# A four-layer adaptive transformer stack in fp32: layers 0 and 1 by halves of the tokens, layer 1's low-rank maps multiplied ahead, and attention's first steps placed among them

## The chip, the core and the metric

The kernel runs on one core of one Trainium2 chip. A core has a matrix engine (TensorE, "PE" in the profile, with its weight loads as "PEld"), three elementwise engines (VectorE "DVE", ScalarE "ACT", GpSimd "POOL") and DMA queues. Each engine works through its own list of instructions in order; semaphores tie them together. Matrix products land in PSUM, eight banks of 128 partitions x 512 fp32 numbers; everything else lies in SBUF. The metric is device time in microseconds of one execution.

## What is computed

There are 8 sequences of 128 tokens with 512 features, so 1024 tokens. Four layers each add to x:

```python
x = x + L0_ffn(L0_cond(x, itok_B_2_6))     # gated MLP with low-rank terms, then routed experts
x = x + L1_ffn(L1_cond(x, itok_B_3_7))     # low-rank map per sequence, then soft-routed experts
x = x + L2_ffn(L2_cond(x, table, lens))    # attention over a paged cache, then a dense layer
x = x + L3_ffn(L3_cond(x, itok_B_0_7))     # routed experts, then 64 small experts

def L0_cond(x): # F = 1376, rank 16, per-sequence A, B
    gate = x @ Wg.T + 0.5 * (x @ Ag.T) @ Bg.T
    up   = x @ Wu.T + 0.5 * (x @ Au.T) @ Bu.T
    h = silu(gate) * up
    return h @ Wd.T + 0.5 * (h @ Ad.T) @ Bd.T

def L0_ffn(x):  # 8 experts of rank 16, the best 2 of them
    w = top2_normalised(softmax(x @ router.T))
    mid = einsum('bsd,edr->bser', x, A) * w[..., None]
    return x @ base.T + 2 * einsum('bser,erd->bsd', mid, B)

def L1_cond(x, ids): return (x @ B[ids].T) @ A[ids].T            # rank 16
def L1_ffn(x):  # 8 experts of rank 16, all of them
    scores = 8 * softmax(x @ Wr.T + br)
    return 2 * einsum('bshr,hor,bsh->bso', einsum('bsd,hrd->bshr', x, A), B, scores)

def L2_cond(x): # 32 query heads, 8 key heads of 128, 512 cached keys + 128 new ones
    q, k = rope(rmsnorm(x @ Wq.T)), rope(rmsnorm(x @ Wk.T)); v = x @ Wv.T
    p = softmax(mask(q @ concat(k_cache[table], k).T / sqrt(128)))
    return (p @ concat(v_cache[table], v)) @ Wo.T
```

L3_cond has the form of L0_ffn with a bias on the logits.

## The kernel before

x is kept transposed, 128 partitions x 4 chunks x 1024 tokens. `TG` = 2 halves of 512 tokens, `NB` = 8 blocks of 128, `DC` = 4 chunks of features, `NF` = 11 chunks of the hidden size. `mm` is one matmul; all matmuls in the profile show the line of such a helper. Tiles come from pools; a pool with `bufs=1` has one buffer for a tag, so the next tile of this tag has to wait until the last one is read. Instructions of an engine can be moved against each other by the scheduler, within their dependencies.

The down projection runs over all tokens for two output chunks at a time, with its low-rank term after the first pair:

```python
for o in range(0, DC, 2):
    wd = st.tile([P, NF, 2 * P], F32, tag="wd", name=f"wd_{o}")      # and its load
    banks = [bank(f"dn_{o}_{j}") for j in range(4)]                   # four quarters of the tokens
    for k in range(2):
        for j in range(4):
            for f in range(NF):
                mmq(banks[j][:, k, :], wd[:fw, f, k * P : (k + 1) * P], h[:fw, f, quarter(j)], ...)
    if o == 0:
        lora_down()                                                   # td, tdm
    ... mmq(banks[j][:, k, :], Bd[...], tdm[slot(j), :], False, True)
    for j in range(4):
        act.copy(y0[:, o : o + 2, quarter(j)], banks[j])
```

The experts of layers 0, 1 and 3 are one function over all 1024 tokens (shortened):

```python
def experts(sm, ps_pool, yT, wmr, tag, topk, mult, bias, wB, base, evac):
    for j in range(NB // 2):
        ps = ps_pool.tile([P, 2, 136], F32, tag="mm", name=f"mid_{tag}_{j}")
        for i in range(2):
            for c in range(DC):
                mm(ps[:, i, :], yT[:, c, t0 : t0 + P], wmr[:, c, :], c == 0, c == DC - 1)
        dve.tensor_copy(lg[:, 2 * j : 2 * j + 2, :], ps[:, :, 128:136])   # or + bias
        mids.append(ps)
    dve.tensor_reduce(mx, lg, AX.X, ALU.max)
    dve.tensor_tensor(e, lg, mx..., ALU.subtract)
    act.activation(e, e, AF.Exp)
    if topk:                          # rank of each of the 8 against the other 8: r1, r2, rank
        ...
    ...                               # s: sum, scale, reciprocal; e * s
    for g in range(TG):
        pt = ps_pool.tile([P, 512], F32, tag="mm", name=f"midTp_{tag}_{g}")
        for j in (2 * g, 2 * g + 1):
            dve.tensor_tensor(mw, mids[j][:, :, 0:128], e..., ALU.mult)
            for i in range(2):
                pe.transpose(pt[:, o : o + P], mw[:, i, :], ident)
        act.copy(midT[:, g * 512 : (g + 1) * 512], pt)
    for o in range(DC):
        for g in range(TG):
            ps = ps_pool.tile([P, 512], F32, tag="mm", name=f"eo_{tag}_{o}_{g}")
            if base is not None:
                for c in range(DC):
                    mm(ps, base[:, c, o * P : (o + 1) * P], yT[:, c, tok], c == 0, False)
            mm(ps, wB[:, o * P : (o + 1) * P], midT[:, tok], base is None, True)
            evac(o, tok, ps)          # add_to_x on VectorE, or a copy
```

Layer 1 follows layer 0, and attention follows layer 1:

```python
experts(sm, psp, y0, wmr0, "l0", "probs", 2.0, None, wB0, base0, add_to_x)
for g in range(TG):
    for c in range(DC):
        mm(ps, wa1[:, c, :], x[:, c, tok], c == 0, c == DC - 1)           # t
    block_masked(t1[:, tok], ps, mask1, g)
    for o in range(DC):
        mm(ps, wb1[:, o * P : (o + 1) * P], t1[:, tok], True, True)       # y
        act.copy(y1[:, o, tok], ps)
experts(sm, psp, y1, wmr1, "l1", None, 16.0, br..., wB1, None, add_to_x)
sp.dma_start(kept, x)
y2 = attention(tc, a, x, ident, lens, kvrow, part, ww, ypool, sums, rows, chunks, mm)
```

Attention has 32 steps (4 groups of heads x 8 sequences) with two key heads each, behind a set-up of sines and cosines (`rotary`). In a step:

```python
def gather(n):      # POOL: 4 + 4 indirect DMAs
    kn = kvp.tile([P, 4, nk], F32, tag="kn", name=f"kn_{n}")              # bufs=2
    ...             # cached keys into kn, cached values into vals[n % 2]
def rope(src, n, nh, tabs, tag):
    t = wk.tile(..., tag="ra" + n); u = wk.tile(..., tag="rb" + n)        # bufs=2
    dve.tensor_tensor(t, src, ws..., ALU.mult)
    for lo, hi in ((0, 64), (64, 0)):
        pool.tensor_tensor(u[:, :, lo : lo + 64], src[:, :, hi : hi + 64], wx..., ALU.mult)
    dve.tensor_tensor(t, t, u, ALU.add)
    return t
def project(n):
    ...             # POOL: four table products ts, tx of sine and cosine with the norm weights
    ...             # kv and two q products, copies, squares (sq), sums of squares (ssq)
    act.activation(rs, ssq, AF.Sqrt, bias=eps, scale=1.0 / HD); dve.reciprocal(rs, rs)
    ...             # k and q times rs
    S[n]["k"] = rope(k1, "k", ...); S[n]["q"] = [rope(t, "q", ...) for t in qs]
def turn(n):
    ...             # kTc: cached keys transposed, copied to kT by DVE; kTn: the new keys
    ...             # qTp: queries transposed, copied to qT by ACT          (bufs=4)
def weigh(n, g):    # st: kT x qT, exp on ACT into pT
def mix(n, g, pT):  # av: pT x vals; sums: reciprocal of the row sum; o, on DVE
def leave(n, g, o): # oTp: o transposed, oT on ACT, wo product, added to y2 on DVE

weights(0); gather(0); project(0); turn(0)
last = None
for n, (qd, b) in enumerate(steps):
    for g in range(GK):
        pT = weigh(n, g)
        o = mix(*last) if last else None
        if more and g == 0:
            gather(n + 1); project(n + 1)
        if more and g == 1:
            turn(n + 1)
        if last:
            leave(*last[:2], o)
        last = (n, g, pT)
```

In PSUM, attention has three banks "mm" (kv, q, kTc, kTn, qTp, oTp, wo), three "st" and two "av". Then come layer 2's dense part and layer 3, whose last part multiplies 64 small experts (z, zT, o).

Of the kernel before, what the change touches and what calls it, by code (L numbers as in the profile page):

```python
# [2 lines left out]

# [6 lines left out]
F32 = mybir.dt.float32  # L10
I32 = mybir.dt.int32
AF = mybir.ActivationFunctionType
ALU = mybir.AluOpType
# [4 lines left out]
NB = 8  # L18
# [28 lines left out]
def forward(ctx: ExitStack, tc: tile.TileContext, a: dict, out: bass.AP):  # L47
# [12 lines left out]
    ew = ctx.enter_context(tc.tile_pool(name="ew", bufs=2))  # L60

# [129 lines left out]
    def experts(sm, ps_pool, yT, wmr, tag, topk, mult, bias, wB, base, evac):  # L191

        lg = sm.tile([P, NB, 8], F32, tag="lg", name=f"lg_{tag}")
        mids = []
        for j in range(NB // 2):
            ps = ps_pool.tile([P, 2, 136], F32, tag="mm", name=f"mid_{tag}_{j}")
            for i in range(2):
                t0 = (2 * j + i) * P
                for c in range(DC):
                    mm(ps[:, i, :], yT[:, c, t0 : t0 + P], wmr[:, c, :], c == 0, c == DC - 1)  # L200
            if bias is None:
                dve.tensor_copy(lg[:, 2 * j : 2 * j + 2, :], ps[:, :, 128:136])
            else:
                dve.tensor_tensor(
                    lg[:, 2 * j : 2 * j + 2, :], ps[:, :, 128:136], bias[:, 2 * j : 2 * j + 2, :], ALU.add
                )
            mids.append(ps)
        mx = sm.tile([P, NB], F32, tag="mx", name=f"mx_{tag}")
        dve.tensor_reduce(mx, lg, AX.X, ALU.max)
        e = sm.tile([P, NB, 8], F32, tag="e", name=f"e_{tag}")  # L210
        dve.tensor_tensor(e, lg, mx.unsqueeze(2).to_broadcast([P, NB, 8]), ALU.subtract)
        act.activation(e, e, AF.Exp)
        if topk:

            by = lg if topk == "logits" else e
            me = by.unsqueeze(3).to_broadcast([P, NB, 8, 8])
            other = by.unsqueeze(2).to_broadcast([P, NB, 8, 8])
            r1 = sm.tile([P, NB, 8, 8], F32, tag="r1", name=f"r1_{tag}")
            r2 = sm.tile([P, NB, 8, 8], F32, tag="r2", name=f"r2_{tag}")
            dve.tensor_tensor(r1, other, me, ALU.is_gt)  # L220
            dve.tensor_tensor(r2, other, me, ALU.is_equal)
            dve.tensor_tensor(r2, r2, lower.unsqueeze(1).to_broadcast([P, NB, 8, 8]), ALU.mult)
            dve.tensor_tensor(r1, r1, r2, ALU.add)
            rank = sm.tile([P, NB, 8], F32, tag="rank", name=f"rank_{tag}")
            dve.tensor_reduce(rank, r1, AX.X, ALU.add)
            dve.scalar_tensor_tensor(e, rank, 2.0, e, ALU.is_lt, ALU.mult)
        s = sm.tile([P, NB], F32, tag="s", name=f"s_{tag}")
        dve.tensor_reduce(s, e, AX.X, ALU.add)
        dve.tensor_scalar(s, s, 1.0 / mult, None, ALU.mult)
        dve.reciprocal(s, s)  # L230
        dve.tensor_tensor(e, e, s.unsqueeze(2).to_broadcast([P, NB, 8]), ALU.mult)

        midT = sm.tile([P, NT], F32, tag="midT", name=f"midT_{tag}")
        for g in range(TG):
            pt = ps_pool.tile([P, 512], F32, tag="mm", name=f"midTp_{tag}_{g}")
            for j in (2 * g, 2 * g + 1):
                mw = sm.tile([P, 2, P], F32, tag="mw", name=f"mw_{tag}_{j}", bufs=2)
                dve.tensor_tensor(
                    mw.rearrange("p i (e r) -> p i e r", r=16),
                    mids[j][:, :, 0:128].rearrange("p i (e r) -> p i e r", r=16),  # L240
                    e[:, 2 * j : 2 * j + 2, :].unsqueeze(3).to_broadcast([P, 2, 8, 16]),
                    ALU.mult,
                )
                for i in range(2):
                    o = ((j % 2) * 2 + i) * P
                    pe.transpose(pt[:, o : o + P], mw[:, i, :], ident)
            act.copy(midT[:, g * 512 : (g + 1) * 512], pt)
        for o in range(DC):
            for g in range(TG):
                ps = ps_pool.tile([P, 512], F32, tag="mm", name=f"eo_{tag}_{o}_{g}")  # L250
                tok = slice(g * 512, (g + 1) * 512)
                if base is not None:
                    for c in range(DC):
                        mm(ps, base[:, c, o * P : (o + 1) * P], yT[:, c, tok], c == 0, False)
                mm(ps, wB[:, o * P : (o + 1) * P], midT[:, tok], base is None, True)
                evac(o, tok, ps)

# [14 lines left out]
    wB0 = load_small(ew, "wB0", [P, D], a["wB0"], tag="wB")  # L272
    with c0:
# [14 lines left out]
        def transposed(t, n, name):  # L288
            k = (n + P - 1) // P
            r = w0.tile([P, k, P], F32, tag=name, name=name)  # L290
# [82 lines left out]

        AdT = transposed(Ad, FF, "AdT")
# [11 lines left out]
        for o in range(0, DC, 2):  # L386
            os_ = slice(o * P, (o + 2) * P)
            wd = st.tile([P, NF, 2 * P], F32, tag="wd", name=f"wd_{o}")
            sp.dma_start(
                wd[:, 0 : NF - 1, :],  # L390
                a["WdT"][0 : (NF - 1) * P, os_].rearrange("(f p) o -> p f o", p=P),
            )
            last = FF - (NF - 1) * P
            sp.dma_start(wd[:last, NF - 1, :], a["WdT"][(NF - 1) * P : FF, os_])
            banks = [bank(f"dn_{o}_{j}") for j in range(4)]
            for k in range(2):
                for j in range(4):
                    for f in range(NF):
                        fw = min(P, FF - f * P)
                        mmq(  # L400
                            banks[j][:, k, :], wd[:fw, f, k * P : (k + 1) * P], h[:fw, f, quarter(j)],
                            k == 0 and f == 0, False,
                        )
            if o == 0:
                lora_down()
            for k in range(2):
                for j in range(4):
                    mmq(banks[j][:, k, :], Bd[slot(j), (o + k) * P : (o + k + 1) * P], tdm[slot(j), :], False, True)
            for j in range(4):
                act.copy(y0[:, o : o + 2, quarter(j)], banks[j])  # L410


    ww = ctx.enter_context(tc.tile_pool(name="ww", bufs=2))


    with ExitStack() as c1:
        w1 = c1.enter_context(tc.tile_pool(name="w1", bufs=1))
        sm = c1.enter_context(tc.tile_pool(name="sm", bufs=1))
        psp = c1.enter_context(tc.tile_pool(name="psp1", bufs=8, space=PSUM))

        base0 = load_small(ww, "base0", [P, DC, D], chunks(a["base0"]), tag="wo")
        wa1 = load_small(w1, "wa1", [P, DC, P], chunks(a["wa1"]))
        wb1 = load_small(w1, "wb1", [P, D], a["wb1"])
# [863 lines left out]
```

## Time and profile before

| | |
|---|---|
| median of three runs | 1821.38 us (1819.6 to 1821.45) |
| profiled execution, span | 1817.8 us |
| mean granted TensorE clock | 0.981 |
| GpSimd busy | 511.6 us |
| DMA | 81.27 MB, mean 45 GB/s |

By the timeline of TensorE, the gate, up and down projections fill the span up to 268 us, the experts of layer 0 and all of layer 1 go on to 359 us, and the loop of attention is in its stride from about 430 us.

In the page, "busy" is the time that an engine spends in instructions; the list of slices shows it in tenths for 40 equal parts of the span. The list of waits says which engine stood before which tile, for whom, and how long in all. A line of the timeline gives start and length in us, engine, line of the program, operation, output tile <- input tiles, partitions x elements, and how many were merged; in brackets is the idle time before it and who ended it. Each fp32 matmul leaves two records.

### The profile page before, as it was taken

How to read it: one execution, taken by the hardware profiler on the slowest of the kernel's cores; microseconds unless marked ns; L12 is line 12 of the kernel's file. 1: busy time of each engine (PE TensorE's matmuls, PEld its weight loads, DVE VectorE, ACT ScalarE, POOL GpSimd, SP SyncE). 2: the span in 40 equal slices, each digit the busy share in tenths (PEclk: the TensorE clock that was granted, in tenths of full speed). 3: DMA queues.
4: the chain of work that ended last, by engine and by line, in shares of the span. 5: the costliest groups of instructions: out<-in, count | busy, mean ns of one | idle time of the engine just before them, and what ended most of it. 6: DMA issues, size and time to landing. Idle time of an engine off the chain costs nothing.

```text
span 1817.8 us, 18511 instructions
## 1 busy us (share of the span) xinstructions
PE 1735.1 (95%) x7537; PEld 1078.9 (59%) x7537; DVE 553.7 (30%) x1130; ACT 528.0 (29%) x876; POOL 511.6 (28%) x597
## 2 busy tenths in 40 slices
PE   7999998859999999999999999999999999989878
PEld 6888884425666556666556565565655656654433
DVE  1000002333433334433344333443334433331121
ACT  1000000134333344333443333433334333410110
POOL 1000000053543434434344343443434442100000
PEclk9999999969999999999999999999999999989999
DMA  7110004120010122001020210002110010010001
GB/s 254 35 34 5 1 22 158 64 70 24 24 33 26 47 82 70 29 30 34 25 93 28 77 32 27 24 26 80 52 53 24 24 35 15 33 50 1 0 0 48
DMA packets 50621, 81.27 MB, mean 45 GB/s; under 512 B 8768, under 2 KB 28288, under 8 KB 50400
## 3 DMA queue, kind: packets, MB, share of 16 engines
q1 hardware_dynamic: 37568, 43.54, 7.3%
q0 software_dynamic: 12960, 36.47, 6.2%
q8 instruction: 61, 1.00, 0.2%
q14 instruction: 32, 0.26, 0.0%
HBM read 75.79 MB, written 4.19 MB: 44 GB/s over the span
## 4 chain that ended last, share of the span: by engine, by line
PE 79%; DVE 3%; POOL 1%; issue 1%; ACT 1%; DMA 0%; POOLq 0%; DVEq 0%; ACTq 0%
PE av L52 15%; PE st L52 15%; PE wo L52 13%; PE q L52 12%; PE kv L52 6%; PE eo_l L52 4%; PE h L52 2%; PE qTp L646 2%; PE z L52 2%; PE oTp L688 2%; PE o L52 2%; PE kTc L636 1%; PE mid_l L52 1%; POOL kn L571 1%; PE y L52 0%
## 5 line engine op out<-in xcount | busy, mean ns | idle before, releaser
L52 PEld LDWEIGHTS av<-vals,pT 128*128 128x128 f32 x2560 | 305.7, 192 | 48.2 <-issue 48.0
L52 PE MATMUL av<-vals,pT 128*128 128x129 f32 x2560 | 311.6, 275 | 3.0 <-DVE sums L677 3.0
L52 PE MATMUL st<-qT,kT 128*128 128x512 f32 x640 | 303.0, 597 | 0.0
L52 PE MATMUL wo<-wo,oT 128*128 128x512 f32 x512 | 236.7, 605 | 1.0 <-ACT oT L690 0.9
L659 ACT ACTIVATE pT<-st,hide 128x512 f32<-128x512 f32 x256 | 175.8, 688 | 173.2 <-PE st L52 173.1
L52 PE MATMUL q<-wq,x 128*128 128x512 f32 x512 | 224.9, 592 | 0.0
L575 POOL DMA_INDIRECT vals<-in_v_cache,kvrow x128 | 121.6, 950 | 291.6 <-PE av L52 260.8
L52 PEld LDWEIGHTS st<-qT,kT 128*128 128x128 f32 x640 | 115.1, 192 | 109.2 <-issue 109.0
L52 PEld LDWEIGHTS wo<-wo,oT 128*128 128x128 f32 x512 | 92.1, 189 | 137.4 <-issue 92.1
L52 PEld LDWEIGHTS q<-wq,x 128*128 128x128 f32 x512 | 97.3, 190 | 122.5 <-issue 122.5
L532 POOL TENSOR_TENSOR rb_k<-k,txk 128x128 f32<-128x128 f32 x64 | 53.5, 855 | 348.1 <-DVE k L625 348.1
L571 POOL DMA_INDIRECT kn<-in_k_cache,kvrow x128 | 123.2, 963 | 58.7 <-issue 29.5
L532 POOL TENSOR_TENSOR rb_q<-qs,txq 128x256 f32<-128x256 f32 x128 | 123.4, 993 | 0.0
L52 PE MATMUL kv<-wkv,x 128*128 128x512 f32 x256 | 115.4, 593 | 0.8 <-DVE x L259 0.8
L602 DVE TENSOR_REDUCE ssq<-sq_q 128x4 f32<-128x512 f32 x64 | 43.8, 686 | 200.8 <-ACT sq_q L601 200.8
L770 POOL MEMSET eps<- 128x1 f32 x1 | 0.1, 99 | 337.4 <-PE eo_l L52 337.4
L648 ACT COPY qT<-qTp 128x512 f32<-128x512 f32 x64 | 37.5, 586 | 197.6 <-PE qTp L646 195.4
L313 PE MATMUL gu<-x,wg 128*128 128x256 f32 (+1 forms) x352 | 83.0, 390 | 9.9 <-DMA x<-in_xT 9.9
L313 PEld LDWEIGHTS gu<-x,wg 128*128 128x128 f32 (+1 forms) x352 | 66.6, 192 | 23.5 <-issue 13.6
L697 DVE TENSOR_TENSOR y<-wo,y 128x512 f32<-128x512 f32 x56 | 38.3, 684 | 136.5 <-PE wo L52 136.5
L617 ACT COPY qs<-q 128x512 f32<-128x512 f32 x64 | 37.4, 586 | 146.0 <-issue 78.0
L313 PE MATMUL gu<-x,wu 128*128 128x256 f32 (+1 forms) x352 | 79.6, 379 | 0.0
(262 smaller groups left out, 1814.0 us busy)
## 6 DMA issues: line engine op xcount, KB each, us to landing
wq<-in_WqT SPq DMA_DIRECT2D x8, 1024.0 KB, 5.3
wo<-in_WoT SPq DMA_DIRECT2D x8, 1024.0 KB, 5.2
wg<-in_WgT SPq DMA_DIRECT2D x10, 256.0 KB, 2.9
wu<-in_WuT SPq DMA_DIRECT2D x10, 256.0 KB, 3.6
wd<-in_WdT SPq DMA_DIRECT2D x2, 1280.0 KB, 14.3
x<-in_xT SPq DMA_DIRECT2D x2, 1024.0 KB, 9.0
base<-in_base SPq DMA_DIRECT2D x2, 1024.0 KB, 5.4
wkv<-in_WkT SPq DMA_DIRECT2D x4, 512.0 KB, 4.1
```

The source lines that it names most:

```text
L52: pe.matmul(o, lhsT, rhs, start=start, stop=stop)
L313: pe.matmul(o, lhsT, rhs, start=start, stop=stop, skip_group_check=True)
L532: pool.tensor_tensor(u[:, :, lo : lo + 64], src[:, :, hi : hi + 64], wx[:, lo : lo + 64].unsqueeze(1).to_broadcast([P, nh, 64]), ALU.mult,)
L571: pool.indirect_dma_start(out=kn[:, c, :], out_offset=None, in_=kc, in_offset=off)
L575: pool.indirect_dma_start(out=v[:, c, 1 : nk + 1], out_offset=None, in_=vc, in_offset=off)
L602: dve.tensor_reduce(ssq[:, at : at + nh], sq, AX.X, ALU.add)
L617: act.copy(t, ps.rearrange("p (h d) -> p h d", d=HD))
L646: pe.transpose(ps[:, i * P : (i + 1) * P], s["q"][g][:, i, :], ident)
L648: act.copy(t, ps)
L659: act.activation(pT[:, c, :, :].rearrange("p i t -> p (i t)"), ps, AF.Exp, bias=s["hide"][:, c : c + 1] if c < 4 else 0.0,)
L688: pe.transpose(ps[:, i * P : (i + 1) * P], o[:, i, :], ident)
L697: dve.tensor_tensor(y2[:, b, :], ps, y2[:, b, :], ALU.add)
```

## The change

It cuts the token range in two halves from the down projection on, so that work of one half can stand beside the routing of the other. Down projection, expert functions and layer 1 become small steps that the main program sets in a chosen order. In layer 1 the second low-rank matrix and the experts' first matrix (with the router) are multiplied once into w11 (128 x 136), so that y is no longer formed. Attention's projection of steps 0 and 1, its first gather and the transposes of the first cached keys are set between the steps of layers 0 and 1; the sine and cosine set-up goes ahead of the down projection. For that, attention's pools must be live while layers 0 and 1 run, and several of its buffers become single.

Cut to its core:

```diff
+    sm  = ctx.enter_context(tc.tile_pool(name="sm", bufs=2))
+    wop = ctx.enter_context(tc.tile_pool(name="wop", bufs=2))
+    rp  = ctx.enter_context(tc.tile_pool(name="rp", bufs=1))
...
-    def experts(sm, ps_pool, yT, wmr, tag, topk, mult, bias, wB, base, evac):
+    def experts(tag, wmr, topk, mult, bias, wB, base, yT, evac, mid_of=None):
+        def mids(g, bank):      # 4 blocks; PSUM is copied to m by ACT
+            ...
+                    for k, (l, r) in enumerate(ops):      # mid_of: one product, else DC
+                        mm(ps[:, i, :], l, r, k == 0, k == len(ops) - 1)
+                act.copy(m[:, 2 * j : 2 * j + 2, :], ps)
+        def route(g):           # the same operations on half the tokens, up to mw (bufs=1)
+        def mix(g, bank):       # 4 transposes, copy to T[g]
+        def outs(g, os, bank):  # eo for the given output chunks
+        return mids, route, mix, outs
...
+    wmr1 = load_small(ew, "wmr1", ...); wB1 = ...; br = rows("br", 8)     # ahead of the gates
+    base0 = load_small(wop, "base0", [P, DC, D], chunks(a["base0"]), tag="wo")
...                              # behind the gates:
+        wb1 = load_small(w0, "wb1", [P, D], a["wb1"], tag="Ag")
+        wb1T = transposed(wb1, D, "wb1T", tag="AgT")
+        ps = psp.tile([P, 136], F32, tag="mm", name="w11p")
+        for c in range(DC):
+            mm(ps, wb1T[:, c, :], wmr1[:, c, :], c == 0, c == DC - 1)
+        w11 = const.tile([P, 136], F32, tag="w11", name="w11")
+        act.copy(w11, ps)
+        rot = rotary(tc, rp, w0, lens, part, rows)
...
+        halves = [down(0, 0), down(0, 1)]
+        lora_down()
+        lora_out(halves)
+        halves = [down(1, 0)]
+        mids0(0, psp_bank)
+        route0(0)
+        halves.append(down(1, 1))
+        lora_out(halves)
...                              # attention's pools and PSUM banks are taken here
+        mix0(0, small_bank)
+        outs0(0, (0, 1), large_bank)
+        mids0(1, small_bank)
+        route0(1)
+        outs0(0, (2, 3), large_bank)
+        mix0(1, small_bank)
+        outs0(1, (0, 1), large_bank)
+        adapt(0)                 # t of half 0, masked
+        outs0(1, (2, 3), large_bank)
+        mids1(0, small_bank)     # from t and w11
+        route1(0)
+        att.begin()              # weights(0), gather(0), turn_cached(0): kTc
+        adapt(1)
+        mix1(0, small_bank)
+        outs1(0, range(DC), large_bank)
+        mids1(1, small_bank)
+        route1(1)
+        att.project(0)
+        mix1(1, small_bank)
+        outs1(1, range(DC), large_bank)
+        sp.dma_start(kept, x)
+        y2 = att.run()           # out_weights(0), gather(1), project(1), turn(0), then the loop
...                              # in attention:
-            u = wk.tile([P, nh, HD], F32, tag="rb" + n, name=f"rb_{tag}")
+        u = wk.tile([P, nh, HD], F32, tag="rb" + n, name=f"rb_{tag}", bufs=1)
-            kn = kvp.tile([P, 4, nk], F32, tag="kn", name=f"kn_{n}")
+        kn = kvp.tile([P, 4, nk], F32, tag="kn", name=f"kn_{n}", bufs=1)
-                sq = wk.tile([P, nh, HD], F32, tag="sq", name=f"sq_{tag}")
+            sq = wk.tile([P, nh, HD], F32, tag="sq", name=f"sq_{tag}", bufs=1)
-                t = wk.tile([P, REP * P], F32, tag="qT", name=f"qT_{n}_{g}", bufs=4)
+            t = wk.tile([P, REP * P], F32, tag="qT", name=f"qT_{n}_{g}", bufs=3)
-            o = wk.tile([P, REP, HD], F32, tag="o", name=f"o_{n}_{g}")
+        o = wk.tile([P, REP, HD], F32, tag="o", name=f"o_{n}_{g}", bufs=1)
-            oT = wk.tile([P, REP * P], F32, tag="oT", name=f"oT_{n}_{g}")
+        oT = wk.tile([P, REP * P], F32, tag="oT", name=f"oT_{n}_{g}", bufs=1)
...                              # layer 3:
-    experts(sm, psp, x, wmr, "l3", "logits", 2.0, bias3, wB, base, to_y)
+    mids, route, mix, outs = experts("l3", wmr, "logits", 2.0, bias3, wB, base, x, to_y)
+    for g in range(TG):
+        mids(g, bank)
+        route(g)
+    for g in range(TG):
+        mix(g, bank)
+        outs(g, range(DC), bank)
```

The second branch of the program, an attention for rows whose sums leave the range of fp32, is changed in its buffers only and doesn't run on these inputs.

## The prediction

> **What bounds the kernel now.** I read the page's busy times, then its list of 40 slices, then the waits of TensorE, and last the timelines around the longest of them.
>
> ```profile
> PE 1735.1 (95%) x7537; PEld 1078.9 (59%) x7537; DVE 553.7 (30%) x1130; ACT 528.0 (29%) x876; POOL 511.6 (28%) x597
> ...
> PE   7999998859999999999999999999999999989878
> ...
> PEclk9999999969999999999999999999999999989999
> ```
>
> TensorE is busy 95% of 1817.8 us. Its holes are at the start, in slices 8 to 10 (45.4 us each, so from 318 to 454 us) and in layer 3 at the end; slice 9 is the only one with a low granted clock. So a gain has to come from work taken off TensorE or from those holes. The waits of TensorE over the whole span name them (columns: total us, times, longest):
>
> ```profile
> PE midTp_l L246 <- DVE mw_l L238: 16.2, 4, 7.6
> PE zT L1212 <- DVE zg L1204: 13.9, 8, 8.0
> PE kTn L640 <- DVE ra_k L538: 11.5, 1, 11.5
> PE gu L313 <- DMA x<-in_xT: 9.9, 1, 9.9
> PE pT L1119 <- DVE p L1114: 5.5, 1, 5.5
> PE kTc L636 <- DMA kn<-in_k_cache,kvrow: 4.3, 4, 2.8
> PE qTp L646 <- DVE ra_q L538: 3.9, 2, 2.9
> PE av L52 <- DVE sums L677: 3.0, 1, 3.0
> PE mid_l L52 <- ACT y L410: 2.1, 1, 2.1
> ```
>
> The 16.2 us of midTp are 7.6 in layer 0, 2.7 in layer 1 and 6.0 in layer 3: TensorE waits for the routing on VectorE. kTc, kTn, qTp and av are the start of attention. The waits on zT, gu and pT are not touched by the change. From 430 us on, attention runs 38.05 us a step (the wo products of consecutive steps start at 428.8, 466.6 and 504.7 in the chain), with no listed wait of TensorE. But one wait of the weight load stands at every step, and one of VectorE (window 440 to 1640 us):
>
> ```profile
> PEld qTp L646 <- DVE kT L637: 5.2, 28, 0.2
> ```
> ```profile
> DVE ra_q L538 <- POOL rb_q L532: 17.3, 28, 0.6
> ```
>
> VectorE therefore has no slack there: it waits for GpSimd's rb_q, then works without a pause until the copies to kT, and the next transposes wait for the PSUM bank that such a copy empties.
>
> **What the Trainium skill says.** "TensorE: Matmul & The Clock Gate", section "What's actually happening": an idle window of about 3.4 us puts TensorE at half clock until it has been busy for as long. The trace agrees:
>
> ```profile
> 388.59 0.66 PE L640 MATMUL kTn<-ident,ra_k 128*128 128x128 f32 x2 [11.50 <-DVE ra_k L538]
> 392.12 1.09 PE L646 MATMUL qTp<-ident,ra_q 128*128 128x128 f32 x4 [2.88 <-DVE ra_q L538]
> 394.19 1.09 PE L646 MATMUL qTp<-ident,ra_q 128*128 128x128 f32 x4 [0.97 <-DVE ra_q L538]
> 395.06 5.16 PE L52 MATMUL st<-qT,kT 128*128 128x512 f32 x6
> ```
>
> Six records of st take 5.16 us here; at 1177.6 us, in the middle of attention, six take 2.74. Thus a removed gap pays more than its length. "GPSIMD Engine Reference", section "Key points": GpSimd shares its SBUF interfaces with VectorE when VectorE reads two SBUF inputs. The trace agrees: the VectorE add onto ra_q takes 1.20 us while rb_q runs and 0.76 with little beside it. "Perfetto Trace Analysis", section "Identifying the Most-Contended Engine", warns that matmul busy time misleads; hence I argue from waits and from starts, not from the 95%.
>
> **Part 1, work on TensorE.** A 128x512 product is two records and costs 0.86 us (4 of t in 3.45 us by the chain), a 128x136 product 0.232 us (32 of mid in 7.43), a transpose 0.11 (8 in 0.9). Layer 1's y products go: 8 x 0.86 = 6.9, shown as two bouts of 3.54. Its mid falls from 32 products to 8: 7.4 to 1.9. New are four transposes of wb1 (0.45) and four 128x136 products for w11 (0.93). Sum: -14.5 + 3.3 = -11.2 us, all on the path. The other matmuls stay, in another order.
>
> **Part 2, waits in layers 0 and 1 and the start of attention.** From 267 to 430 us TensorE waits 2.1 (mid for y0), 7.6 (routing 0), 1.6 (y for the masked t, twice), 2.7 (routing 1), 0.8 (kv for x), 4.3 (kTc), 11.5 (kTn), 3.9 (qTp) and 3.0 (av): 37.5 us. Half clock adds to this. The first quarter of mid ends 3.8 us after its start, the others 1.86 apart: 1.9. Behind the 7.6 wait, eight transposes and two records of eo last from 286.8 to 290.6, 3.8 instead of 8 x 0.11 + 2 x 0.43 = 1.7: 2.1. Behind kTn: st 5.0 against 2.6, and some 0.7 in the transposes: 3.1. Together 7.1 us.
>
> What fills these holes afterwards: routing of half 0 (VectorE 279.3 to 287.1 for 1024 tokens, with halved r operations some 5 us) lies under the second down half (44 products of 256 columns, 9.4 us, and the low-rank part, 1.2). Routing of half 1 lies under two eo outputs (8.6 us), layer 1's under t of half 1 (3.4) and kTc (0.9). The rope of step 0, about 14 us from the last q to ra_q, lies under four eo products, kv and q of step 1: 3.4 + 3.4 + 6.9 + 0.5 = 14.2 us. GpSimd's gathers, which in the kernel before stand from 359 to 388 us in front of rb_k and make the 11.5 us, can start when h is dead, some 50 us before their use.
>
> New waits, stepwise. w11p needs the copy of wb1T on ScalarE, behind the last four Silu (they run from 182.97 to 184.17): copy 0.59, so TensorE, which finishes the transposes at about 183.35, goes on at 184.75: 1.4. At the change of the PSUM pool up to four y0 copies (2.1 us in the kernel before) must end: 2.0. mw of layer 1 late by 0.5, masked t 0.25, x for kv 0.45, two copies 0.2: 1.4. Start of st 0.5, rope 1.0. For what I can't see, 3.0. Sum: +9.3.
>
> **Part 3, layer 3.** Its experts are now halved too, but without other work between: routing 0 is hidden only by the mids of half 1 (3.7 us). A wait of 6.0 becomes about 1.5, and the 2.1 us of half clock behind it (1689.2 to 1693.0) should go: -6.6.
>
> **Part 4, buffers of attention.** To make room, kn, rb, sq, o and oT become single and qT goes from 4 to 3. kn, sq, o, oT and qT are each read by the time the next is written, by the order of the steps: kn is gathered one step ahead instead of two, 38 us. rb_q is different. In the kernel before:
>
> ```profile
> 1179.82 3.86 POOL L532 TENSOR_TENSOR rb_q<-qs,txq 128x256 f32<-128x256 f32 x4
> ```
> ```profile
> 1181.89 1.20 DVE L538 TENSOR_TENSOR ra_q<-ra_q,rb_q 128x512 f32<-128x512 f32 x1 [0.62 <-POOL rb_q L532]
> 1183.02 1.21 DVE L530 TENSOR_TENSOR ra_q<-qs,tsq 128x512 f32<-128x512 f32 x1
> 1184.15 0.68 DVE L697 TENSOR_TENSOR y<-wo,y 128x512 f32<-128x512 f32 x1
> 1184.75 0.76 DVE L538 TENSOR_TENSOR ra_q<-ra_q,rb_q 128x512 f32<-128x512 f32 x1
> ```
>
> The third and fourth rb_q run during the first add. With one buffer they start only at that add's end, about 1183.0; two take 1.8 to 2.0, so 1184.9 to 1185.1 with the semaphore, where VectorE came for them at 1184.75. A table product of GpSimd moves into the hole, and the first add may end 0.2 sooner for less contention. VectorE's second add then starts 0.1 to 0.45 later, I take 0.27, and the kT copies and qTp go with it, one for one, as shown above. Over 31 steps: +8.4 us (3 to 14).
>
> **Sum.** -11.2 - 37.5 - 7.1 - 6.6 + 9.3 + 8.4 = -44.7; 1821.4 - 44.7 = 1776.7, say 1776 us.
>
> **Rivals.** (a) The single rb_q costs more than I take, 0.5 to 0.7 us a step: 15 to 22 us, total 1783 to 1790. For it: VectorE has no slack, and contention is hard to foresee. Against: GpSimd idles meanwhile. (b) The holes are filled only in part: VectorE now carries routing, adds onto x and the rope of steps 0 and 1 in one order, and an operation that waits blocks those behind it. Each such case is 2 to 5 us; three make 1786. For it: the reciprocal of rs stands behind three adds onto x that need layer 1's second half. (c) The attention loses nothing, and the filling is complete: 1764. (d) Earlier loads of base0, wmr1 and wB1 (1.5 MB, some 5 us at the first slice's 254 GB/s) come ahead of the second gate weights: they are needed at 30.8 us and were issued at 12.4, so this should be hidden; wd moves later in exchange. At worst +3.
>
> **Range and chances.** Low end 1762: (c). High end 1794: (a) and part of (b). 2% faster is 1785.0, 8 us above my number: I give that 0.70, within 2% 0.28. For slower by 2% everything gained would have to be lost in the loop, over 2.5 us a step: 0.02.
>
> **What would show it.** TensorE's kTn wait of 11.5 gone and kTc without a wait on a gather; midTp in layer 0 without a wait and in layer 3 near 1.5; one wait of about 1.4 on w11p; granted clock full from 270 to 400 us; steady attention beginning some 50 us earlier; steps at 38.3 us instead of 38.05, with "qTp <- kT" near 0.45 instead of 0.2. A step of 38.05 refutes part 4, one above 38.6 makes (a). Long waits of kTn or qTp would say that part 2 failed.

## The result and the profile after

The changed kernel takes 1767.78 us (median of four runs, 1767.04 to 1768.26) beside 1821.41 for the kernel before (four runs). The ratio is 0.9707, with a 95% interval of 0.969 to 0.9723. The prediction was 1776, with 1762 to 1794 as its range.

First the page of the changed kernel: the busy times, and TensorE's slices and clock (44.2 us a slice here).

```profile
PE 1714.6 (97%) x7485; PEld 1068.8 (61%) x7485; DVE 532.3 (30%) x1146; ACT 526.7 (30%) x883; POOL 500.2 (28%) x597
...
PE   5999999999999999999999999999999999989978
...
PEclk8999999999999999999999999999999999989989
```

The holes of the kernel before lie in slices 7 to 9 of its page, 272.7 to 409.0 us (the prediction counts one too far: 8 to 10, from 318 to 454). They are filled, and the slice at clock 6 is gone. In exchange the first slice has fallen from 7 to 5. The waits of TensorE over the whole span name the cause (columns as before: total us, times, longest; the waits on x, zT and pT are as they were and left out):

```profile
PE gu L338 <- DVE tgm L345: 8.5, 1, 8.5
...
PE midTp_l L263 <- ACT y L455: 1.7, 1, 1.7
PE midTp_l L263 <- DVE mw_l L252: 1.3, 1, 1.3
PE w11p L53 <- ACT wb1T L323: 1.2, 1, 1.2
```

The waits on kTc, kTn, qTp and av no longer appear, nor does any other of layers 0 and 1. The 1.7 stands at the change of the PSUM pool, the 1.3 is in layer 3. The 8.5 us on tgm are new, and nothing in the prediction's sum stands for them.

Five points that both kernels pass cut the span into stretches. They are read from the timelines and the first and last starts of a tile's instructions: the end of the gates (182.9 us before, 193.3 after), the last low-rank product of the down projection (267.4, 286.0), the first wo product (428.6, 384.1), the last one (1607.1, 1561.2) and the end of the span (1817.8, 1766.1). Beside the measured differences stand the prediction's terms, sorted into the same stretches: the new order puts half of layer 0's mids (3.7 us) and the w11 product (1.4) ahead of the second point.

| stretch | predicted, us | measured, us |
|---|---|---|
| start to the end of the gates | 0 | +10.4 |
| to the last low-rank product of down | +6.5 | +8.2 |
| to the first wo | -53.0 | -63.1 |
| first to last wo (steps of attention) | +8.4 | -1.4 |
| to the end (layers 2 and 3) | -6.6 | -5.8 |
| sum | -44.7 | -51.7 |

Against the terms the stretches are off by +12.9 us (the first two and the last) and by -19.9 (the other two). That the sum is off by only 7.0 is in part luck. The experiments take the stretches one by one.

### The profile page after: what moved, and what is told of

Its sections match the earlier page's. It is cut to its first block, busy times and chain, and to the rows that moved or that the text cites. A ratio compares the mean times of both kernels' runs of the same rounds, so it can differ in the third digit from the quotient of the medians.

```text
span 1766.1 us, 18518 instructions
## 1 busy us (share of the span) xinstructions
PE 1714.6 (97%) x7485; PEld 1068.8 (61%) x7485; DVE 532.3 (30%) x1146; ACT 526.7 (30%) x883; POOL 500.2 (28%) x597
## 4 chain that ended last, share of the span: by engine, by line
PE 96%; DVE 2%; DMA 1%; ACT 1%; SPq 0%; issue 0%; POOLq 0%; ACTq 0%; DVEq 0%
PE av L53 16%; PE st L53 16%; PE wo L53 13%; PE q L53 13%; PE gu L338 10%; PE kv L53 6%; PE dn L338 5%; PE eo_l L53 4%; PE h L53 2%; PE z L53 2%; PE qTp L723 2%; PE kTc L708 2%; PE oTp L766 2%; PE o L53 2%; PE midp_l L53 1%; DMA x<-in_xT 0%
## 5 line engine op out<-in xcount | busy, mean ns | idle before, releaser
L53 PEld LDWEIGHTS av<-vals,pT 128*128 128x128 f32 x2560 | 305.6, 192 | 45.0 <-issue 44.7
L338 PEld LDWEIGHTS gu<-x,wg 128*128 128x128 f32 (+1 forms) x352 | 67.7, 195 | 23.6 <-issue 13.2
L754 DVE RECIPROCAL sums<-av 128x2 f32<-128x2 f32 x128 | 21.3, 166 | 192.2 <-PE av L53 192.2
```

Source lines behind the costliest of these rows:

```text
L53: pe.matmul(o, lhsT, rhs, start=start, stop=stop)
L338: pe.matmul(o, lhsT, rhs, start=start, stop=stop, skip_group_check=True)
```

## The experiments

Times are medians; the kernel before took 1820.6 to 1821.8 us beside them. "Against the changed kernel" means against 1767.8.

**e1: the loss at the start.** In the changed kernel VectorE's timeline shows what stood ahead of tgm (columns: start, duration, operation; in brackets the idle time before it and what ended it):

```profile
32.77 0.69 DVE L826 TENSOR_TENSOR ang<-pos,inv_freq 128x512 f32<-128x512 f32 x1 [17.20 <-DMA inv_freq<-in_inv_freq]
...
39.51 0.42 DVE L345 TENSOR_TENSOR tgm<-t,half 128x256 f32<-128x256 f32 x1
```

And TensorE's timeline of the same kernel shows the price:

```profile
39.98 1.24 PE L338 MATMUL gu<-tgm,Bg 32*128 32x256 f32 x8 [8.46 <-DVE tgm L345]
...
42.00 4.23 PE L338 MATMUL gu<-x,wg 128*128 128x256 f32 x12
```

Rotary's tables, which the kernel before made behind layer 1, have moved to the start. Their first operation waits for a small load that is issued behind large ones; tgm, ready to run since about 30.4 us, stands behind it and sixteen more. Behind the wait TensorE runs at half clock: the three bouts from 39.98 to the end of the one at 42.00 last 6.55 us in all, the same three in e1 4.18.

```diff
     table = ints("block_table", NB * 16)
+    tables = {n: rows(n, w) for n, w in (("inv_freq", 64), ("q_norm", HD), ("k_norm", HD))}
...
-        rot = rotary(tc, rp, w0, lens, part, rows)
+        rot = rotary(tc, rp, w0, lens, part, tables)
```

(inside rotary, the three rows are taken from `tables`)

> The changed kernel, with one thing moved: the three rows that the rotary tables are made of (inv_freq, q_norm, k_norm, 320 numbers each copied to all partitions) are loaded ahead of the big loads, right behind the block table. VectorE's order stays as it is: the rotary operations still stand ahead of tgm. My theory of the 10.4 us lost by the end of the gates (182.89 before, 193.32 after): VectorE works in order, the angle product came ahead of tgm and waited 17.2 us for inv_freq, so tgm, the first low-rank operand, came 8.5 us late, and TensorE fell to half clock behind the wait. Then the wait of 8.5 on tgm should go, the gates should end at 183 to 186 us, and the time fall by 8 to 11 us, to 1757 to 1760. Rival: the larger loads (base0, wmr1, wB1) hold the queues, and x or the first gate weights or Bg come late whatever VectorE does; then the gates still end at 190 us or later and the time stays within 3 us of 1768. A second rival: the rotary work itself, some 24 VectorE operations of about 0.5 us ahead of tgm, delays tgm without any wait on a load; then 2 to 6 us are gained, not 8.

Measured: 1757.44 us (1755.19 to 1759.09), 10.3 less than the changed kernel; ratio to before 0.9645 (0.9632 to 0.9658). The wait on tgm is gone, and VectorE's timeline of e1 has tgm here:

```profile
31.45 0.42 DVE L346 TENSOR_TENSOR tgm<-t,half 128x256 f32<-128x256 f32 x1 [6.42 <-PE t L339]
```

VectorE now waits for TensorE, not the other way round: the rotary work fits in ahead (15.0 to 25.0 us). Down begins at 188.2 us instead of 197.4. Both rivals fall. The large loads come early in e1 too, and cost a wait of 0.7 on wg (1.8 in e2).

**e2: the wait at the PSUM pool, in e1's kernel.**

```diff
         halves.append(down(1, 1))
+        mix0(0, psp_bank)
         lora_out(halves)
+        outs0(0, (0, 1), psp_bank)
...
-        mix0(0, small_bank)
-        outs0(0, (0, 1), large_bank)
```

> The kernel of e1, and the first mix of layer 0 with its first two outputs is set ahead of the change of PSUM pool. In the changed kernel TensorE waits 1.7 us there, until ScalarE's four copies of y0 have emptied the old banks, and 1.15 for the copy of the transposed wb1 remains. If that wait is only a matter of where it stands, it falls under 8.6 us of outputs: 1 to 1.7 us less than e1. Rival: the new pool now has to wait for the additions onto x as well, and the wait only moves: within 0.5 us of e1.

Measured: 1755.87 us (1755.54 to 1757.78), ratio 0.9642 (0.9629 to 0.9655): 1.6 below e1's median, but the intervals overlap. In the trace, the 1.7 of midTp has become 0.9 before the second half's mids, so 0.8 of it is saved. More comes from the clock. In e1's timeline the same wait put TensorE at half speed (granted clock 0.58 from 279 to 286 us):

```profile
278.94 1.12 PE L264 MATMUL midTp_l<-ident,mw_l 128*128 128x128 f32 x4 [1.70 <-ACT y L456]
279.85 6.12 PE L53 MATMUL eo_l<-y,base 128*128 128x512 f32 x8
```

In the changed kernel, behind the same wait, the same two bouts take 0.66 and 3.60, and behind e2's 0.9 the clock stays full. That is 2.9 us between the profiled executions of e1 and e2; the longer wait on wg takes 1.1 back. e2 has the lowest median here, below both kernels of the comparison.

**e3: two buffers for rb again** (the tag is that of rb_k and rb_q).

```diff
-        u = wk.tile([P, nh, HD], F32, tag="rb" + n, name=f"rb_{tag}", bufs=1)
+        u = wk.tile([P, nh, HD], F32, tag="rb" + n, name=f"rb_{tag}")
```

> The changed kernel with two buffers for rb_q again. The prediction said that the single buffer costs 0.27 us a step; then the step falls from 37.98 to 37.7 and the time by 8 us. The trace of the changed kernel points the other way: with one buffer GpSimd and VectorE alternate, the first add onto ra_q takes 0.93 us instead of 1.20 and the product behind it 0.68 instead of 1.21, and the step is 37.98 instead of 38.05. If this is the cause, the step goes back to 38.05 and the time rises by some 2 us. Rival: the 0.07 comes from something else in the loop (gathers one step ahead, three buffers for qT): the step stays at 37.98 and the time within 0.7 us.

Measured: 1768.83 us (1768.07 to 1774.25), 1.0 more than the changed kernel. From the first wo to the last it takes 1179.6 us (384.7 to 1564.3), the changed kernel 1177.1 (384.1 to 1561.2): +2.5, as the theory of overlap says, and opposite to the prediction. In the traces of this case the same stretch takes 1176.1 to 1177.1 us wherever rb has one buffer (seven kernels) and 1178.1 to 1179.6 wherever it has two (seven kernels). The groups of VectorE between 460 and 1500 us show why (busy time, mean ns of one, idle before and its releaser). The changed kernel, then e3:

```profile
L602 DVE TENSOR_TENSOR ra_q<-qs,tsq 128x512 f32<-128x512 f32 x54 | 44.0, 814 | 0.0
L610 DVE TENSOR_TENSOR ra_q<-ra_q,rb_q 128x512 f32<-128x512 f32 x54 | 43.5, 806 | 35.1 <-POOL rb_q L604 35.1
```

```profile
L602 DVE TENSOR_TENSOR ra_q<-qs,tsq 128x512 f32<-128x512 f32 x54 | 58.2, 1078 | 0.0
L610 DVE TENSOR_TENSOR ra_q<-ra_q,rb_q 128x512 f32<-128x512 f32 x54 | 52.9, 979 | 16.1 <-POOL rb_q L604 16.1
```

With one buffer VectorE waits 19 us longer for rb_q, over 27 steps. But its products and adds are 14.2 and 9.4 us shorter: 23.6 us given back. In a step of the changed kernel the order of starts is this:

```profile
756.88 0.93 DVE L610 TENSOR_TENSOR ra_q<-ra_q,rb_q 128x512 f32<-128x512 f32 x1 [0.62 <-POOL rb_q L604]
757.73 0.68 DVE L602 TENSOR_TENSOR ra_q<-qs,tsq 128x512 f32<-128x512 f32 x1
757.89 1.79 POOL L604 TENSOR_TENSOR rb_q<-qs,txq 128x256 f32<-128x256 f32 x2 [0.63 <-DVE ra_q L610]
759.72 0.69 DVE L610 TENSOR_TENSOR ra_q<-ra_q,rb_q 128x512 f32<-128x512 f32 x1 [0.70 <-POOL rb_q L604]
```

The product starts 0.16 us ahead of rb_q and takes 0.68, though rb_q then runs beside it. In the kernel before (the lines in the prediction) it starts while rb_q is running and takes 1.21. So it counts which of the two starts first, more than that both run.

**e5: the single buffer for rb alone, in the kernel before.**

```diff
-            u = wk.tile([P, nh, HD], F32, tag="rb" + n, name=f"rb_{tag}")
+            u = wk.tile([P, nh, HD], F32, tag="rb" + n, name=f"rb_{tag}", bufs=1)
```

> The kernel before, with one buffer for rb_q and rb_k and nothing else. The prediction's part 4 says 38.05 to 38.3 us a step, 8 us more in all. The theory that less overlap of GpSimd and VectorE makes VectorE's operations shorter says 37.98 a step, some 2 us less. Rival: 38.05 and no difference.

Measured: 1818.99 us beside 1820.75, ratio 0.9992 (0.9984 to 1.0): the time by itself hardly tells it from noise. The trace has it more clearly: first to last wo 1176.1 us (430.7 to 1606.8) instead of 1178.5, so -2.4. The first step begins later (first wo at 430.7 instead of 428.6; the waits on qTp and av at the start are 8.1 us instead of 6.9), and that takes most of it back. The means of the two groups fall from 1078 and 975 ns to 807 and 811. So the single buffer by itself is the cause, in both kernels.

**e4: attention's first steps put back behind layer 1.**

```diff
-        att.begin()
...
-        att.project(0)
...
         outs1(1, range(DC), large_bank)
+        att.begin()
+        att.project(0)
```

> The changed kernel, with attention's first steps put back behind layer 1: the load of the first weights, the first gather, the transposes of the cached keys and the projection of step 0 are called after the last output of layer 1. The halves and the single product of layer 1 stay. The prediction put 22.7 us of waits (kTc 4.3, kTn 11.5, qTp 3.9, av 3.0) and 3.1 of half clock on this start, less 1.5 of new waits. If it is the setting among layer 1 that removes them, 8 to 20 us come back (the gathers can still start early, so less than all 24), with waits on kTn, qTp or av. Rival: it is GpSimd's free time and the common pools that let the gathers start early, and the order matters little: under 4 us.

Measured: 1769.79 us (1768.03 to 1772.72), 2.0 more than the changed kernel. One wait is new among TensorE's waits:

```profile
PE qTp L723 <- DVE ra_q L610: 1.5, 1, 1.5
```

The rival holds. The gathers still begin at 287.7 us, and the compiled order puts kTc, kv and the first of q among layer 1's products on its own, as TensorE's timeline of e4 shows:

```profile
336.00 0.60 PE L708 MATMUL kTc<-ident,kn 128*128 128x128 f32 x4
...
341.46 3.60 PE L53 MATMUL kv<-wkv,x 128*128 128x512 f32 x8
...
346.28 3.70 PE L53 MATMUL eo_l<-midT_l,wB 128*128 128x512 f32 x8
```

So the place of the calls is worth some 2 us. What the interleaving itself is worth this run does not say, since most of it is still there.

**e9: e4, and the projection of step 1 back behind the first scores.**

```diff
         out_weights(0)
-        gather(1)
-        project(1)
         turn(0)
...
-                if more and g == 0 and n:
+                if more and g == 0:
                     gather(n + 1)
                     project(n + 1)
```

> The kernel of e4, and in attention's own beginning the projection of step 1 is called behind the first scores of step 0 again, as in the kernel before, and no longer ahead of the transposes of step 0's new keys and queries. e4 gave back only some 2 us, with a single wait of 1.5 on qTp. One theory: it is the projection of step 1 (kv 3.4 and q 6.9 us) that hides the rope of step 0; without it TensorE waits 8 to 12 us on kTn and qTp, then 3 on av, and works at half clock behind it: +10 to +15 us against e4. Rival: the waits in the kernel before were made by the gathers, which stood ahead of rb_k on GpSimd and which the new pools let start at 287 us; with them early the rope alone is short, and the wait is 3 to 6 us: +4 to +8.

Measured: 1788.84 us (1787.42 to 1790.25), 19 more than e4, above even the first theory. Two of TensorE's waits in e9:

```profile
PE kTn L717 <- DVE ra_k L610: 8.3, 1, 8.3
...
PE av L53 <- DVE sums L754: 3.4, 1, 3.4
```

With 2.4 on qTp these make 14.1 us, and 12.6 more than e4's 1.5. From 360 to 380 us the granted clock is 0.66 instead of 1.00: six records of st take 4.83 us, in the changed kernel 2.84. The projection of step 1, 10.3 us of ready work, is what hides most of the rope. Not all of the 19 need be its worth: at the wait of 1.7 at the PSUM pool, which both kernels have, the profiled execution of e9 fell to half clock (the eight records of eo behind it take 6.16 us) and that of e4 did not (3.60). That is 3.0 us of the difference between these two executions; without it the first theory's 15 is nearly met.

**e12: that order alone, in the kernel before.**

```diff
         project(0)
+        gather(1)
+        project(1)
         turn(0)
...
-                if more and g == 0:
+                if more and g == 0 and n:
                     gather(n + 1)
                     project(n + 1)
```

> The kernel before, with one thing changed: attention calls the gather and the projection of step 1 ahead of the transposes of step 0's new keys and queries. e9 says that this order is worth 19 us in the changed kernel. Layers 0 and 1, the memory of the pools and the late gathers stay. If the 10.3 us of kv and q simply fill the wait of 11.5 on kTn, that wait falls to 1 to 3 us, kTc's wait and av's 3.0 go as well, and the half clock behind them: 16 to 20 us less. Rival: the late gathers (GpSimd until 388 us) hold kTn and qTp regardless of what TensorE does meanwhile, and 10.3 us of work in front of them are all there is to gain, with the half clock still there: 8 to 12 us less.

Measured: 1804.33 us, ratio 0.9908 (0.9891 to 0.9924): -16.3. The wait of 11.5 on kTn has become 1.3, that of av is gone, but a wait of 6.3 on kTc has come. ScalarE's timeline gives its reason:

```profile
387.71 0.59 ACT L617 COPY qs<-q 128x512 f32<-128x512 f32 x1 [10.47 <-POOL rb_q L532]
```

The copy of step 1's first q has no buffer until rb_q of step 0 has read one of the two, and rb_q stands behind GpSimd's gathers. kTc needs the PSUM bank that this copy empties. The rival is right that the late gathers still hold something and that half clock stays (six records of st take 4.73 us), but the total lies with the first theory.

**e10: the early gathers alone, in the kernel before.**

```diff
+    vp = ck.enter_context(tc.tile_pool(name="vp", bufs=1))    # vals
+    kvp = ck.enter_context(tc.tile_pool(name="kvp", bufs=2))  # kn
...
+    early = {n: gather(n) for n in range(2)}
     with ExitStack() as c1:                                   # layers 0 and 1
```

> The kernel before, with the buffers of the gathered keys and values (kn, vals) in memory of their own and the gathers of steps 0 and 1 called ahead of layers 0's experts. All else stays: whole experts, the y products, rotary's tables behind layer 1, the order of attention's steps. In the kernel before GpSimd idles from 21 to 358.8 us, until the last output of layer 1 frees the memory, and then makes gathers until 388. If this queue makes the waits on kTc (4.3) and most of that on kTn (11.5), both fall: -10 to -15 us with the half clock behind them. Rival: rotary's 9 us of VectorE work (359.4 to 368.2), which waits for the same memory, and the rope itself hold TensorE as long: -4 us, that of kTc alone.

Measured: 1811.04 us, ratio 0.9942 (0.9926 to 0.9959): -10.1, the edge of the first theory. The gathers now begin at 268.2 us, as soon as the down projection frees the memory, and kTc waits for nothing. kTn still waits 8.4, as the rival says: GpSimd can begin on its products of sine and cosine at 369.7 only, and the gathers of step 2 (373.2 to 378.8) again stand in front of rb_k. With e12 this makes -26.4, added up; the prediction had 22.7 of waits and 3.1 of half clock there. No run puts just these two together, and as both shorten the wait on kTn, the sum can be too large.

**e6: layer 1's two maps as one product, alone, in the kernel before** (the edit is shortened).

```diff
-                mm(ps, wb1[:, o * P : (o + 1) * P], t1[:, tok], True, True)   # y1, 4 outputs
+        # wb1T = transposed wb1; w11 = wb1T x wmr1, once
-            sm, psp, y1, wmr1, "l1", ...
+            sm, psp, t1, w11, "l1", ...      # one product for the mid instead of four
```

> The kernel before, with the two low-rank maps of layer 1 as one product and nothing else: no y products of layer 1, 8 instead of 32 products for its mid, and four transposes and four 128x136 products for the joint map. The prediction's part 1 says -14.5 + 3.3 less a copy of 0.6 to wait for at most... in numbers: -11.2, or -10.6 with that wait. The waits for the copies of y (1.6 for the masked t) may shrink as well: down to -13. Rival: TensorE was waiting for VectorE or ScalarE there anyway, and the work taken off turns into waits: -3 to -6.

Measured: 1810.95 us, ratio 0.9942 (0.9927 to 0.9957): -9.8. From the last low-rank product to the first wo it takes 151.5 us instead of 161.2, -9.7. Part 1 is confirmed with 1.4 less than its -11.2. Of this, 1.2 is clock: layer 1's last sixteen records of eo take 8.27 us instead of 7.11, at a granted clock of 0.85 (341 to 350 us) instead of 1.00.

**e8: layer 0's first routing not set among the down projection.**

```diff
-        mids0(0, psp_bank)
-        route0(0)
         halves.append(down(1, 1))
         lora_out(halves)
+        mids0(0, psp_bank)
+        route0(0)
```

> The changed kernel, with the mids and the routing of layer 0's first half called behind the whole down projection instead of between its quarters. If calling them there is what hides the routing, a wait of 4 to 6 us and some half clock return: +5 to +8 us. Rival: halving alone does it, because the compiled order can set base products of the other outputs into the hole: under +2 us.

Measured: 1767.02 us, ratio 0.9704 (0.9689 to 0.9718), the same as the changed kernel. TensorE's timeline of e8:

```profile
287.99 6.28 PE L53 MATMUL eo_l<-y,base 128*128 128x512 f32 x14 [0.47 <-issue]
294.10 0.60 PE L263 MATMUL midTp_l<-ident,mw_l 128*128 128x128 f32 x4
```

Fourteen records of base products, which need no routing, were compiled into the hole, which the routing of half the tokens makes 5.5 us long (288.0 to 293.5). Where the source calls it matters nothing. Why the compiled order of the kernel before left its 7.6 us empty is not shown; the base weights had landed by 273.9 us there, so it was not for lack of them.

**e7 and e11: the low-rank products of down.** A bout of 16 such records (rows 32, columns 256) takes 1.15 us in the kernel before and 2.00 in the changed one, as the two timelines have it:

```profile
228.20 1.15 PE L313 MATMUL dn<-tdm,Bd 32*128 32x256 f32 x16
```
```profile
241.42 2.00 PE L338 MATMUL dn<-tdm,Bd 32*128 32x256 f32 x16
```

e7 keeps the kernel before and reorders within a bout:

```diff
-            for k in range(2):
-                for j in range(4):
+            for k, j in ((0, 0), (0, 1), (1, 0), (1, 1), (0, 2), (0, 3), (1, 2), (1, 3)):
```

> The kernel before, with the low-rank products of the down projection in the order that the halves bring: two quarters, both outputs, then the other two quarters, instead of four quarters in turn. The same 16 products in each of two bouts. They stand in four groups of 32 rows. If products in different row groups run beside each other, four at a time before and two now, a bout goes from 1.15 us to some 2.0 and the time rises by 1.7 us. Rival: order is nothing to them, and the longer bouts of the changed kernel come from the clock or from missing records: 1.15 stays.

Measured: 1.16 us a bout, 1820.91 us against 1820.75, ratio 0.9999 (0.999 to 1.0007). My expectation was wrong: the order within a bout of four row groups does nothing. e11 therefore gives each bout two groups only:

```diff
-            for k in range(2):
-                for j in range(4):
-                    ... products with wd, then lora_down, then those with Bd, over all j
+            for jj in ((0, 1), (2, 3)):
+                ... the same, over j in jj
```

> The kernel before, with the down projection's inner work by pairs of quarters: the products and then the low-rank products of quarters 0 and 1, then those of quarters 2 and 3. The work is the same; there are four bouts of 8 low-rank records in place of two of 16, and each bout uses two groups of 32 rows only. e7 changed the order within a bout of four groups and the bout stayed at 1.16 us for 16 records, so a plain order does not matter. If the number of row groups in a bout does (the changed kernel's bouts have two groups and take 2.00 us for 16 records), a bout of 8 records takes 1.0 us instead of 0.58, and the down projection 1.7 us more in all. Rival: the longer bout of the changed kernel has another cause: 0.55 to 0.6 us for 8 records.

Measured: 1820.46 us against 1820.62, ratio 0.9998 (0.9989 to 1.0006). Each of the four bouts reads like this in TensorE's timeline:

```profile
208.52 1.13 PE L313 MATMUL dn<-tdm,Bd 32*128 32x256 f32 x8
```

Half the records in the same time: what counts is the number of records in one row group. Four of them take 1.13 to 1.16 us (e11, the kernel before, e7), eight take 2.00 (the changed kernel). Down takes 2.4 us longer in e11, and nothing of it is left in the total. The wait on y behind it falls from 2.1 to 1.2, and with this shorter wait TensorE keeps its full clock:

```profile
270.74 7.68 PE L52 MATMUL mid_l<-wmr,y 128*128 128x136 f32 x64 [1.16 <-ACT y L411]
```

In the kernel before the same bout takes 9.35 us behind its wait of 2.12, with a granted clock of 0.83 from 270 to 280 us. That gives 0.9 and 1.7 back.

## Why the prediction was right, and where it failed

**Part 1 (work, -11.2).** Right: -9.8 by e6. Its sum is not quite that of its terms: those listed give -12.4 (6.9 and 5.5) and +1.4 (0.45 and 0.93), so -11.0; -14.5 and +3.3 do not follow from them.

**Part 2 (waits removed, -37.5, half clock -7.1, new waits +9.3).** All the waits that it lists are gone, and the third stretch fell by 10.1 us more than its terms. Of new waits 7.9 were set aside for this stretch and 1.7 came, at the PSUM pool (predicted 2.0); the small ones of layer 1, the late rope and the 3.0 "for what I can't see" did not. That is 6.2. Another 1.7 is kTc at half clock: eight transposes took 2.7 us besides their waits in the kernel before and 1.04 now. Another 0.7 is six av records that no longer stand ahead of the first wo. The last 1.5 is open. (The wait on w11p, 1.2 for 1.4, lies in the second stretch.)

The mechanism was right in part. Of the 14.2 us of work that the prediction laid over the rope, the 10.3 of step 1's kv and q carry most: -16.3 in the kernel before (e12). The early gathers are worth -10.1 by themselves (e10), but they did not make the whole wait of 11.5 on kTn, as the prediction has it: 8.4 of it stay in e10. Where the program calls attention's first steps and the first routing matters little (e4 2 us, e8 nothing), because the compiled order finds the ready work by itself. What the two halves are worth in layers 0 and 1 no run takes apart: their waits are gone from the trace, and the rest is argued. One size was far off without harm: the second half of down that covers the first routing was put at 9.4 us, and its 88 records take 19.17.

**Part 3 (layer 3, -6.6).** Right: the wait is 1.3, and from the first mid to the first q of layer 3 it takes 44.3 us instead of 51.3, -7.0. The stretch as a whole gave 5.8, as the part behind that q took 1.1 longer; 0.7 of this is eight z records behind the wait of 8.0 on zT, 5.76 us instead of 5.04.

**Part 4 (single rb_q, +8.4).** Wrong in sign. The step that failed is "VectorE's second add then starts 0.1 to 0.45 later". Counted from the start of the first add, the second starts after 2.84 us in the changed kernel (756.88 to 759.72) and after 2.86 in the kernel before (1181.89 to 1184.75): 0.02 earlier, not 0.27 later. The first add takes 0.93 instead of 1.20 and so frees the buffer sooner, two pieces of rb_q then take 1.79, the short end of "1.8 to 2.0", and the second add takes 0.69 instead of 0.76. A step is 37.98 us (wo at 445.06 and 483.04) instead of 38.05, and e3 and e5 put -2.5 and -2.4 us on the buffer alone. The prediction had named the sharing of SBUF interfaces, and allowed 0.2 for less contention only in passing; this was the larger effect. (Its add of 0.76 us was not one "with little beside it": GpSimd's txq and tsq ran beside it from 1184.51 to 1185.83. But no rb_q did.) Its own test, "a step of 38.05 refutes part 4", was met from the other side.

**Rival (d), "at worst +3".** Wrong by size and by cause: +10.4. It looked for lateness in the large loads. These cost 0.7 to 1.8 us of wait on wg in e1 and e2, within its bound. What hurt was rotary's small load behind them, in front of tgm in VectorE's order. The working did not list rotary's tables as moved, although the diff does. e1 takes 10.3 of it back.

**Missed.** The low-rank products of down, +0.85 us for each of two bouts (e11). This 1.7 is the whole difference between the second stretch and its term.

## What to carry to other kernels

When work moves earlier, look at the engine that runs it: an operation that waits for a late load holds everything behind it on that engine, here 8.5 us of TensorE for a row of 64 numbers. Before you weave stages together by hand, look for the one block of ready work and the one shared buffer that the long wait hangs on; here, each in the kernel before, one change of order gave 16.3 us and early gathers into buffers of their own 10.1. Where two engines slow each other, a wait that sets them apart also shortens what follows: estimate it with the durations of the engines apart, not with those measured side by side.

## What the runs showed of the hardware

A VectorE product of 128x512 took 1.21 us where it started while GpSimd's rb_q was running and 0.68 where rb_q started 0.16 us after it; between 460 and 1500 us a single buffer lowered its mean from 1078 (e3) to 814 ns. The Trainium skill names the sharing ("GPSIMD Engine Reference", section "Key points"); the size is from these runs.

Products of 32 rows ran beside each other in different row groups: 16 records took 1.15 us over four groups and 2.00 over two, and 8 over two took 1.13.

A wait of 1.7 us left TensorE at full clock in the changed kernel and at half clock in e1, 2.9 us dearer. A wait of 1.16 left it at full clock (e11), and those of 2.12 and 2.84 ahead of mid and kTc in the kernel before were followed by half clock. The Trainium skill ("TensorE: Matmul & The Clock Gate", section "What's actually happening") speaks of an idle window of about 3.4 us; by these runs a shorter gap can be enough, and need not be. The gaps of 1.7 follow a bout of 32-row products of 2.00 us; whether such products count as idle no run here shows.
